# Moving four pieces of work inside the rows of a two-step graph layer

## The chip, the cores and the metric

The kernel runs on one core of a Trainium2 chip, in one launch. The metric is device time in microseconds (us). The engines named below are TensorE (PE, with its weight loads as PEld), VectorE (DVE), ScalarE (ACT), GpSimd (POOL) and SyncE (SP, which issues most DMAs). Each engine runs its own instructions in order and waits for the others through semaphores.

## The reference

3327 nodes with 256 features each; the adjacency matrix has about five entries a row. After a layer norm and a ReLU, two steps of two sums run side by side, and a last layer norm closes. Cut to what matters:

```python
h = maximum(layernorm(x), 0)
R = adj + eye;  R = R / R.sum(-1)            # sparse graph sum
Xf = Xa = h;  Z = 0
for n in range(2):
    probs = softmax((Xa @ W1.T @ W2.T) @ (Xa @ W3.T).T)     # N x N
    keep  = the largest probabilities of each row, until their sum reaches 0.9
    A     = probs * keep / (probs * keep).sum(-1)
    Xf = R @ Xf
    Xa = A @ Xa
    Z  = Z + Xf @ U1[n].T + Xa @ U2[n].T
out = x + layernorm(h + Z)
```

## The kernel before

The nodes are padded to 26 blocks of 128 (`NT`), and a "row" below is one block of 128 nodes against all 3328. For each row of a step the kernel makes the logits on PE and their exponentials on ACT (`weights`, four parts of 832 columns, tile `e`), guesses a threshold with passes over the whole row on ACT (`measured`, L660 to L762, each pass 128x3328 into `ja`), searches the exact threshold on DVE (`settle`, L765: one masked copy of the row at L772, the eight largest of 20 segments at L777, rounds of MAX8 and MATCH_REPLACE at L784 and L788, and the masked row itself at L814), turns the masked row block by block on PE with copies on ACT (`Sums.turn`, L862 and L864), and sums it with the features on PE (`Sums.sum`, L876).

The guess uses a "law", a mean and a variance for each query. In the first step `law_once` makes it row by row: a matmul (L525) and a copy on ACT (L527), and then a product on DVE (L533) and five small operations on POOL (L536 to L540). `weights` calls the first half after the first exponential and the second half after the second.

The graph sum is sparse. In the first step DVE scans the whole adjacency matrix in pieces (`listed`: a DMA into `at`, and a TENSOR_REDUCE at L906) to list the entries of each row; rows from 7 on come in seven pieces of at most 128x512, and each call asks for the next piece's DMA ahead of its own reduction, in two buffers. POOL gathers the listed rows with indirect DMAs (L973 and L990), and `spread` (L1213) sums them: five matmuls into the PSUM tile `pr` (L998), and on DVE L1222, L1224, L1226, L1227 (which reads `pr`) and L1230, then a store to `vx`. `pr` has one buffer, and `first_end` (L1021) uses it next, for the matmuls of L1036.

The order on each engine is written by hand. The loop at the end runs over the rows `i`, and each row has seven slots `k`. A slot's string names generators by letters, and each letter runs one of them to its next `yield`: `m` measured, `d` settle, `c` the rest of the last row's settle, `s` graph sum, `w` logits and exponentials of row i+2, `a` a list piece, `i` the chain that closes a list, `p` and `h` the packing of lists, `g` a gather, `e` and `f` the ends of rows, `b` the products ahead of the first step. `PLAN` (L1249) holds the strings of a common row, `BEGIN` and `OPEN` those of the first rows. In the first step the turning comes behind a slot's letters, in the second in front of them; the sums come last. In the second step slot 1 sums two blocks and slot 2 none (`BLOCKS`), and in slot 2 the first two blocks of the newly masked row are turned. At the end every instruction is tied to the one before it in its engine's queue, so this order is the order on the chip. A gather is also tied to the ACT instruction written last before it.

Of the kernel before, what the change touches and what calls it, by code (L numbers as in the profile page):

```python
# [328 lines left out]
HALVES = 7  # L329
# [17 lines left out]
def guess_graph_layer(ctx, tc, x, adj, w1t, w2t, w3t, u1t, u2t, ln_g, ln_b, out, flag):  # L347
# [18 lines left out]
    valid = lambda t: 0 <= t < NT  # L366
# [148 lines left out]
    def asked(t):  # L515
        qT = tpool.tile([P, P], F32, tag="qT", name="qT", bufs=3)
        for rows in (low, high):
            nc.sync.dma_start(qT[rows], query_of(t))
        return qT

    def law_once(step, t, copy=S.copy):

        pq = ps_t.tile([P, 4, P], F32, tag="pt", name="pq")
        pm = pq[:, 1:3, :].rearrange("p a b -> p (a b)")[:, : 2 * DA + 2]
        PE.matmul(pm, query_of(t), qm[query_at(t), step, :], start=True, stop=True)  # L525
        mq = small.tile([P, 2 * DA + 2], F32, tag="mq", name="mq", bufs=2)
        copy(mq, pm)  # L527
        yield


        ms = small.tile([P, 9], F32, tag="ms", name="ms")
        col = lambda k: ms[:, k : k + 1]
        V.scalar_tensor_tensor(mq[:, : DA + 1], mq[:, : DA + 1], 1.0, mq[:, DA + 1 :], ALU.mult, ALU.mult,  # L533
                               accum_out=col(1))
        minus = mq[:, 2 * DA + 1 :]
        G.tensor_tensor(col(2), col(1), half[:, 1:2], ALU.pow)  # L536
        G.tensor_scalar(ms[:, 3:7], of_s[:, step, :], col(2), 1.0e-4, ALU.mult, ALU.add)
        G.tensor_scalar(col(7), col(1), 0.5, minus, ALU.mult, ALU.subtract)
        G.tensor_scalar(col(7), col(7), 0.25, LNY[step] - 0.25 * math.log(0.1 / N), ALU.mult, ALU.add)
        G.tensor_scalar(col(8), col(1), minus, col(4), ALU.subtract, ALU.add)  # L540
        return col
# [31 lines left out]
    def law_of(t):  # L573

        return lambda k: law[:, {7: 1, 8: 4}.get(k, k), t : t + 1]

    def weights(step, t, live, known=True):

        r = dict(Z=rec[:, step, 3, t : t + 1])
        qT = asked(t)  # L580
        yield
        r["ms"] = law_of(t) if known and step else early.get(t)
        lawful = law_once(step, t) if known and not step else none
        r["e"] = e = es[(2, 3, 0, 1, 4, 5)[t % 6] if step else t % 4]
        r["za"] = za = small.tile([P, CUT + 1], F32, tag="za", name="za")
        live[step, t] = r
        w = HALF * P
        wd = w // CUT
        pls = {}

        def product(n):
            pls[n] = pl = ps_l.tile([P, 2, 512], F32, tag="pl", name="pl")
            for a in range(2):
                p = slice(a * DA, (a + 1) * DA)
                PE.matmul(pl[:, a, :wd], qT[p, :],  # L595
                          keys_of(step, a).rearrange("p a b -> p (a b)")[:, n * wd : (n + 1) * wd],
                          start=True, stop=True)

        for n in range(CUT):
            c = n * wd  # L600
            if n not in pls:
                product(n)
            pl = pls.pop(n)
            if n < CUT - 1:
                S.activation(e.rearrange("p (a n) -> p a n", a=2)[:, :, c : c + wd], pl[:, :, :wd],  # L605
                             AF.Exp, accum_out=za[:, n : n + 1])
                if known and not step and n < 2:
                    r["ms"] = returned(lawful) if n else next(lawful)
                if known and step and n == CUT - 2:
                    product(n + 1)  # L610
                yield
            else:
                S.activation(e.rearrange("p (a n) -> p a n", a=2)[:, :, c : w - 1], pl[:, :, : wd - 1],
                             AF.Exp, accum_out=za[:, n : n + 1])
                S.activation(e[:, w - 1 : w], pl[:, 0, wd - 1 : wd], AF.Exp, accum_out=za[:, n + 1 :])
                if step:
                    r["chain"] = guessing(r)

    def guessing(r):

        r["col"] = col = lambda k, g=small.tile([P, 18], F32, tag="g", name="g"): g[:, k : k + 1]
        ms = r["ms"]
        S.activation(r["za"], r["za"], AF.Copy, accum_out=r["Z"])
        yield
        S.activation(col(0), r["Z"], AF.Ln)
        yield
        S.activation(col(2), col(0), AF.Relu, scale=-0.25, bias=ms(7))
        yield
        S.activation(col(1), col(0), AF.Exp, scale=-1.0, bias=con(5))
        yield  # L630
        S.activation(col(2), col(2), AF.Exp, scale=-1.0, bias=con(9))
        yield
        S.activation(col(3), col(2), AF.Square, bias=con(8))
        yield
        S.activation(col(11), col(2), AF.Square, bias=con(4))  # L635
        S.activation(col(9), col(3), AF.Exp, scale=ms(3), bias=ms(8))

    def guess_of(t):
        for _ in live[1, t]["chain"]:
            yield  # L640
# [16 lines left out]
    def con(k):  # L657
        return one[:, k : k + 1]
# [277 lines left out]
    def chain():  # L936
        while chains:
            if next(chains[0], chains) is chains:
                chains.pop(0)
            yield  # L940
# [133 lines left out]
    def proof():  # L1074
        prove(1)
        yield
        pf = ps_t.tile([P, 4, P], F32, tag="pt", name="pf")
        PE.matmul(pf[:1, 0, :1], fl, ones, start=True, stop=True)
        V.tensor_copy(flag, pf[:1, 0, :1])

    none = iter(())
    chains = []
    own_of, kept, ends = {}, {}, []
    live, ohs, acs, xgs, done, early = {}, {}, {}, {}, [], {}

    def run(work, n=99):
        for _ in range(n):
            next(work, None)

    def returned(work):  # L1090
        while True:
            try:
                next(work)
            except StopIteration as end:
                return end.value
# [29 lines left out]
    lister, product = listed(), products()  # L1125
# [3 lines left out]
    for q in range(HALF + 5):  # L1129
# [31 lines left out]
        if 0 <= q - 1 < HALF:  # L1161
            k, rn = q - 1, scaled.pop(q - 1)
            pt = ps_t.tile([P, 4, P], F32, tag="pt", name="pt")
            for h in range(2):
                t = 2 * k + h
# [70 lines left out]
    def refetch(t):  # L1236
# [8 lines left out]

    ROUNDED = "dsdfdfddfd"
    CLOSED = "zmdmzmzdmmdmdmdmdmd"
    SEARCH = "gmdidsdidadsdg", "gmidpdsdpdidiesa"
    PLAN = (("gmdsssa", "gmcdssa", "edawwpg", *SEARCH, "ohgdeawwqg", "gehmdmdmagq"),  # L1249
            ("llcmnmss", "lms", "lwwnfd", "lcmdssgggg", "fdwmwmqd", "llzmz" + ROUNDED, "l" + CLOSED + "g"))  # L1250

    LAST = {NT - 1: ("cfss", "cn", "nd", "sss", "f" + "d" * 5 + "sdf" + "d" * 11, "ff", ""),
            NT: ("c", "", "", "ff", "ff", "ffv", "f"),
            NT + 1: ("fv", "f", "", "", "f", "f", "f")}
    BEGIN = {-1: ("mba", "mmbba", "mwwbbaa", "bmwwb", "", "", ""),
             0: ("mdbb", "mcdbb", "medbwwbp", "mdbb", "gmpdbwwb", "hgdbgbq", "hgq"),
             1: ("ggmdsssbb", "gmcdgsssbb", "gedbwwbp", "bmsdg", "gmpdeg", "hgdwwqg", "hgemgqo"),
             NT + 1: ("", "weweee", "", "", "", "", ""),
             2: ("gmdsssa", "gmcdssga", "gedawwpg", *SEARCH, "ohgdeawwqg", "gehmdmdmagq")}
    OPEN = {-1: ("mxx", "mxl", "mxlggg", "mgxl", "mwxl", "m" * 7 + "l", "lmlggg"),  # L1260
            0: ("cmmssggg", "lnms", "wwnfd", "cmdss", "fdwmgwmqd", "zmz" + ROUNDED, CLOSED),
            1: ("cmnmss", "ms", "wwnfd", "cmdssgggg", "fdwmwmqd", "zmzg" + ROUNDED, CLOSED + "g")}
    OPEN[2] = OPEN[3] = OPEN[1]
    spacing = itertools.chain(spaced((0, 1)), *(spaced((t,)) for t in range(2, NT)))
    fetching = itertools.chain(*(refetch(t) for t in range(NT)))
# [22 lines left out]
    for step in range(2):  # L1288
        sums = Sums(step, live, xw if step else x0, AHEAD[step])

        for i in range(-1, NT + 2):
            if step == 0 and i == NT - 3:
                begun = [weights(1, t, live, False) for t in range(3)]
            if step == 1 and i == -1:
                ordered.append(len(trace))
            if step == 1 and i == -1:
# [3 lines left out]
                n=work["m"],  # L1300
                c=work["d"],
# [3 lines left out]
                w=later.pop((step, i + 2), none),  # L1305
                z=guess_of(i + 2) if step and i > 0 and valid(i + 2) else none,
                e=first_end(i - 2) if step == 0 and valid(i - 2) else none,
                a=itertools.islice(lister, HALVES) if step == 0 else none, i=chain(),
                p=packed(i + 1) if step == 0 and i >= 0 and valid(i + 1) else none,
                g=fetching if step else spacing if i > -1 else none,  # L1310
                o=asked_for(0, i - 1) if step == 0 and valid(i - 1) else none,
                h=gathered(i) if step == 0 and valid(i) else none,
                b=none if step else product, q=none, v=proof() if step and i == NT else work.get("v", none),
                l=laws(range(3, NT)) if step and i == -1 else work["l"] if step and i == 0 else none,
# [15 lines left out]
            for k in range(PARTS):  # L1330
# [8 lines left out]
                g = PARTS * (i - 1) + k - LATE[step]  # L1339
                summing = valid(g // PARTS)  # L1340
                if step and valid((g + AHEAD[1]) // PARTS):
                    sums.turn(g + (k == 2), min(i, NT - 1))
                for c in ({**OPEN, **LAST} if step else BEGIN).get(i, PLAN[step])[k]:
                    at = len(trace)
# [19 lines left out]
            if step == 1 and i == 0:  # L1364
                for e in es[4:]:
                    G.memset(e[:, N:NP], 0.0)
            for c in ("lcnwqsepb" if i > -1 else "cnwqsepb") if step else "ocmwqseph" + "b" * (i > 0):
                run(work[c])
            if step == 0 and i == NT + 1:
                stores()  # L1370
# [51 lines left out]
```

## Time and profile before

| | us |
|---|---|
| median of 3 runs | 1320.46 |
| lowest and highest | 1314.64, 1323.86 |
| the profiled execution | 1318.03 |
| its span, first to last instruction | 1315.9 |
| mean granted clock of TensorE | 0.982 |
| first step, rows 2 to 25, by the chain of waits | about 130 to 705 |
| between the steps | about 705 to 780 |
| second step | about 780 to 1316 |

The profile is of one execution. A line of its tables has the kernel's line, the engine, the operation, the tiles as out<-in, the shape and the count; then busy time, mean duration in nanoseconds, and the idle time of the engine just before these instructions with what ended it. "issue" means that nothing in the profile shows what ended it. PE's matmuls are pipelined and their ends are modelled, so the spacing of their starts says more than their durations. In a timeline the columns are start, duration, engine, line, operation and tiles, and in brackets the idle time before.

### The profile page before, as it was taken

To read this page: it belongs to the slowest core of one execution; us is meant where nothing else is said; L and a number is where in the kernel's file an instruction comes from. 1 tells how busy PE (TensorE), PEld (TensorE's weight loads), DVE (VectorE), ACT (ScalarE), POOL (GpSimd) and SP (SyncE) were. 2 spreads that over 40 slices of the span, in tenths; PEclk is the share of its full clock that TensorE was granted. 3 is DMA by queue.
4 is the path that set the end of the run, shared out by engine and by line. 5 is a ranking of instruction groups with operands and counts; after the bars stand their busy time and mean duration, and the time that the engine had idled before them with its cause. 6 is when DMAs were issued, how large, how long until landed. Compare 5 with 4: busy or idle time off the path is not lost.

```text
span 1315.9 us, 21931 instructions
## 1 busy us (share of the span) xinstructions
PE 1236.7 (94%) x6292; PEld 935.4 (71%) x6292; DVE 1149.2 (87%) x3830; ACT 1051.4 (80%) x2281; POOL 955.6 (73%) x1201
## 2 busy tenths in 40 slices
PE   5989899999999999999999859999999999999985
PEld 4535677777777777777778537777787777777874
DVE  6867899999999999999685489999999999999993
ACT  5376787787788797887883579999999999999941
POOL 6114888877778878878776367888888888888832
PEclk9999999999999999999999959999999999999998
DMA  7734455555555555553233212222122131221200
GB/s 232 283 127 140 141 147 142 154 154 139 149 145 147 160 148 153 156 139 101 78 97 98 71 48 71 67 71 84 53 85 79 54 89 59 75 85 49 82 21 23
DMA packets 96578, 144.59 MB, mean 110 GB/s; under 512 B 19361, under 2 KB 63008, under 8 KB 96448
## 3 DMA queue, kind: packets, MB, share of 16 engines
q1 hardware_dynamic: 78912, 100.20, 24.3%
q0 software_dynamic: 16640, 42.69, 13.1%
q8 instruction: 52, 0.85, 0.3%
q14 instruction: 78, 0.64, 0.2%
q10 hardware_dynamic: 896, 0.21, 0.1%
HBM read 114.06 MB, written 25.57 MB: 106 GB/s over the span
## 4 chain that ended last, share of the span: by engine, by line
PE 43%; DVE 27%; ACT 22%; issue 3%; DMA 2%; POOL 1%; SPq 0%; ACTq 0%; POOLq 0%; DVEq 0%
PE pa L876 18%; ACT ja L662 11%; PE pl L595 7%; PE pt L862 6%; DVE e L814 5%; DVE cand L777 4%; DVE w L772 3%; DVE fm L906 3%; PE pr L998 3%; ACT e L605 3%; PE pz L1111 3%; PE pz L1036 2%; ACT eT L864 2%; DVE bb L784 2%; DVE x L814 2%
## 5 line engine op out<-in xcount | busy, mean ns | idle before, releaser
L662 ACT ACTIVATE ja<-e,g 128x3328 uint8<-128x3328 f32 x106 | 326.0, 3075 | 0.3
L876 PE MATMUL pa<-xw,eT 128*128 128x256 f32 x1352 | 321.6, 383 | 3.8 <-DVE s L1048 3.8
L876 PE MATMUL pa<-x,eT 128*128 128x256 f32 x1352 | 323.0, 381 | 0.1
L876 PEld LDWEIGHTS pa<-xw,eT 128*128 128x128 f32 x1352 | 251.0, 191 | 49.5 <-issue 13.8
L876 PEld LDWEIGHTS pa<-x,eT 128*128 128x128 f32 x1352 | 243.5, 191 | 26.3 <-ACT xa L885 0.4
L777 DVE MAX8 cand<-w 128x8 f32<-128x168 f32 (+1 forms) x1040 | 253.1, 317 | 0.0
L864 ACT COPY eT<-pt 128x512 f32<-128x512 f32 (+1 forms) x364 | 199.2, 555 | 57.3 <-PE pt L862 50.3
L973 POOL DMA_INDIRECT ac<-in_adj,index x130 | 186.9, 1438 | 60.5 <-issue 29.1
L990 POOL DMA_INDIRECT xg<-bx,index x130 | 180.3, 1387 | 50.3 <-issue 23.8
L862 PE MATMUL pt<-ident,e 128*128 128x128 f32 x1144 | 176.4, 277 | 6.6 <-DVE e L811 2.9
L862 PEld LDWEIGHTS pt<-ident,e 128*128 128x128 f32 x1144 | 139.2, 143 | 60.1 <-issue 36.7
L772 DVE SCALAR_TENSOR_TENSOR w<-e,g 128x3328 f32<-128x3328 f32 x44 | 162.8, 3700 | 0.3
L998 PE MATMUL pr<-xg,ac 128*128 128x257 f32 (+1 forms) x520 | 141.8, 397 | 12.3 <-DVE s L1227 8.1
L990 POOL DMA_INDIRECT xg<-vx,index x130 | 128.4, 987 | 34.2 <-issue 27.6
L814 DVE SCALAR_TENSOR_TENSOR e<-e,rec 128x3328 f32<-128x3328 f32 x40 | 147.2, 3680 | 0.6
L605 ACT ACTIVATE e<-pl 128x832 f32<-128x832 f32 x132 | 114.2, 867 | 27.7 <-PE pl L595 24.3
L998 PEld LDWEIGHTS pr<-xg,ac 128*128 128x128 f32 x520 | 93.8, 195 | 40.1 <-issue 16.9
L595 PE MATMUL pl<-both,qT 64*128 64x416 f32 x416 | 102.2, 549 | 6.9 <-ACT e L605 3.1
L711 POOL TENSOR_SCALAR g<-g,law 128x1 f32<-128x1 f32 x23 | 76.9, 3342 | 22.3 <-ACT g L635 22.1
L906 DVE TENSOR_REDUCE fm<-at 128x4 f32<-128x512 f32 (+1 forms) x133 | 84.7, 637 | 7.9 <-DMA at<-in_adj 5.0
L595 PE MATMUL pl<-after,qT 64*128 64x416 f32 x416 | 89.5, 544 | 0.0
L712 POOL TENSOR_SCALAR g<-g 128x1 f32<-128x1 f32 x26 | 87.0, 3348 | 1.7
(288 smaller groups left out, 2034.9 us busy)
## 6 DMA issues: line engine op xcount, KB each, us to landing
at<-in_adj SPq DMA_DIRECT2D x114, 256.0 KB
cx<-ac SPq DMA_DIRECT2D x26, 320.0 KB
ac<-cx SPq DMA_DIRECT2D x26, 320.0 KB
wide<-in_adj SPq DMA_DIRECT2D x8, 832.0 KB
e<-in_adj SPq DMA_DIRECT2D x6, 832.0 KB
x<-in_x SPq DMA_DIRECT2D x13, 256.0 KB
qT<-both SPq DMA_DIRECT2D x104, 32.0 KB
xr<-in_x SPq DMA_DIRECT2D x26, 128.0 KB
```

What stands on the lines that cost most here:

```text
L595: PE.matmul(pl[:, a, :wd], qT[p, :], keys_of(step, a).rearrange("p a b -> p (a b)")[:, n * wd : (n + 1) * wd], start=True, stop=True)
L605: S.activation(e.rearrange("p (a n) -> p a n", a=2)[:, :, c : c + wd], pl[:, :, :wd], AF.Exp, accum_out=za[:, n : n + 1])
L662: S.activation(ja, e, f, bias=guess, scale=sign, accum_out=total)
L772: V.scalar_tensor_tensor(w, e, col(16), e, ALU.is_lt, ALU.mult, accum_out=d2)
L777: V.max(cand[:, 8 * s : 8 * s + 8], w[:, s * SEG : min(NP, (s + 1) * SEG)])
L814: V.scalar_tensor_tensor(e, e, at(1), e, ALU.is_ge, ALU.mult, accum_out=ra)
L862: PE.transpose(pt[:, j, :], e[:, (j0 + j) * P : (j0 + j + 1) * P], ident)
L864: S.copy(eT[:, :w, :], pt[:, :w, :])
L876: PE.matmul(self.pa, eT[:, c - 4 * k, :], self.xa[:, j, :], start=c == 0, stop=c == NT - 1)
L973: G.indirect_dma_start(out=ac[:, k, :], out_offset=None, in_=rows, in_offset=bass.IndirectOffsetOnAxis(ap=index[:, t, k : k + 1], axis=0), ...
L990: G.indirect_dma_start(out=xg[:, k, :w], out_offset=None, in_=rows, in_offset=bass.IndirectOffsetOnAxis(ap=index[:, t, k : k + 1], axis=0))
L998: PE.matmul(pr[:, :w], ac[:, k, :], xg[:, k, :w], start=k == 0, stop=k == KT - 1)
```

## The change

Four things are moved; no arithmetic is added or removed.

- **The law's product** (first step). The second half of `law_once` is a letter of its own, `u`, near the end of slot 3. Before, it ran in slot 2 with the second `w`.
- **The graph sum** (first step). The last four `s` move from slots 3 and 4 to slots 2 (one), 3 (two) and 4 (one, near its start).
- **The list pieces** (first step). A common row has six `a`, not seven: that of slot 5 is gone, and those of slots 3 and 4 stand at their ends. Rows 0 and 1 get three and four, and the lists end two rows later, in row 22.
- **The first logits** (second step). The two `w` of slot 2 stand at the end of slot 1, after the slot's pass and graph matmul, and ahead of its two blocks of sums.

In row 0 and row 1 a `p` is also called once more in slot 4, where the end of the row ran it before.

```diff
             if n < CUT - 1:
                 S.activation(e.rearrange("p (a n) -> p a n", a=2)[:, :, c : c + wd], pl[:, :, :wd],
                              AF.Exp, accum_out=za[:, n : n + 1])
-                if known and not step and n < 2:
-                    r["ms"] = returned(lawful) if n else next(lawful)
+                if known and not step and n == 0:
+                    r["lawful"] = lawful
+                    next(lawful)
...
+    def law_end(t):
+        live[0, t]["ms"] = returned(live[0, t].pop("lawful"))
+        yield
...
-    SEARCH = "gmdidsdidadsdg", "gmidpdsdpdidiesa"
-    PLAN = (("gmdsssa", "gmcdssa", "edawwpg", *SEARCH, "ohgdeawwqg", "gehmdmdmagq"),
-            ("llcmnmss", "lms", "lwwnfd", "lcmdssgggg", "fdwmwmqd", "llzmz" + ROUNDED, "l" + CLOSED + "g"))
+    SEARCH = "gmdsdidsdiduadg", "gmidpdsdpdidiea"
+    PLAN = (("gmdsssa", "gmcdssa", "edawwspg", *SEARCH, "ohgdewwqg", "gehmdmdmagq"),
+            ("llcmnmss", "lmsww", "lnfd", "lcmdssgggg", "fdwmwmqd", "llzmz" + ROUNDED, "l" + CLOSED + "g"))
...
-             0: ("mdbb", "mcdbb", "medbwwbp", "mdbb", "gmpdbwwb", "hgdbgbq", "hgq"),
-             1: ("ggmdsssbb", "gmcdgsssbb", "gedbwwbp", "bmsdg", "gmpdeg", "hgdwwqg", "hgemgqo"),
+             0: ("mdbb", "mcdbba", "medbwwbp", "mdbba", "gmppdbwwb", "hgdbgbqa", "hgq"),
+             1: ("ggmdsssbba", "gmcdgsssbba", "gedbwwbp", "bmusdga", "gmppdeg", "hgdwwqga", "hgemgqo"),
...
-             2: ("gmdsssa", "gmcdssga", "gedawwpg", *SEARCH, "ohgdeawwqg", "gehmdmdmagq")}
+             2: ("gmdsssa", "gmcdssga", "gedawwspg", *SEARCH, "ohgdewwqg", "gehmdmdmagq")}
...
-            0: ("cmmssggg", "lnms", "wwnfd", "cmdss", "fdwmgwmqd", "zmz" + ROUNDED, CLOSED),
-            1: ("cmnmss", "ms", "wwnfd", "cmdssgggg", "fdwmwmqd", "zmzg" + ROUNDED, CLOSED + "g")}
+            0: ("cmmssggg", "lnmsww", "nfd", "cmdss", "fdwmgwmqd", "zmz" + ROUNDED, CLOSED),
+            1: ("cmnmss", "msww", "nfd", "cmdssgggg", "fdwmwmqd", "zmzg" + ROUNDED, CLOSED + "g")}
...
-                a=itertools.islice(lister, HALVES) if step == 0 else none, i=chain(),
+                a=itertools.islice(lister, 6) if step == 0 else none, i=chain(),
+                u=law_end(i + 2) if step == 0 and i > 0 and valid(i + 2) else none,
...
-            for c in ("lcnwqsepb" if i > -1 else "cnwqsepb") if step else "ocmwqseph" + "b" * (i > 0):
+            for c in ("lcnwqsepb" if i > -1 else "cnwqsepb") if step else "ocmwuqseph" + "b" * (i > 0):
```

## The prediction

> **What bounds the kernel now.** I read the page first: the shares of busy time and the chain that ended last.
>
> ```profile
> PE 1236.7 (94%) x6292; PEld 935.4 (71%) x6292; DVE 1149.2 (87%) x3830; ACT 1051.4 (80%) x2281; POOL 955.6 (73%) x1201
> ...
> PE 43%; DVE 27%; ACT 22%; issue 3%; DMA 2%; POOL 1%; SPq 0%; ACTq 0%; POOLq 0%; DVEq 0%
> ```
>
> No engine is alone on the chain, so a share says little. The next view is the table of windows, cut into rows of the first step (from one start of TensorE's L959 to the next). Columns after the length: busy time of PE, PEld, DVE, ACT, POOL, then granted clock and DMA.
>
> ```profile
> 180.69:205.48 24.79, 23.16 (x122) 17.68 (x120) 23.05 (x78) 19.95 (x47) 20.16 (x23) 1.00 0.56 155
> 426.98:450.07 23.09, 23.09 (x122) 17.69 (x120) 22.95 (x78) 19.73 (x47) 18.80 (x23) 1.00 0.57 157
> ...
> 474.43:498.11 23.68, 23.16 (x121) 17.69 (x120) 23.54 (x78) 19.83 (x47) 19.39 (x23) 1.00 0.56 152
> 498.11:522.48 24.37, 23.96 (x128) 18.22 (x127) 23.63 (x78) 19.95 (x49) 19.75 (x24) 1.00 0.54 151
> 593.82:618.09 24.27, 23.86 (x128) 18.30 (x127) 21.35 (x73) 19.95 (x49) 19.27 (x24) 1.00 0.35 101
> 618.09:640.98 22.89, 22.89 (x121) 17.77 (x120) 18.60 (x61) 19.73 (x47) 17.35 (x21) 1.00 0.31 86
> ```
>
> Short rows and long rows alternate (every second row has the extra Gram matmuls). A short row that waits for nothing takes 23.09 with PE busy throughout. 24.79 and 23.68 are the same work plus a wait. The long row is 24.37 with PE 23.96, and stays 24.27 when the list pieces have ended and DVE has fallen to 21.35. So PE is the floor, and DVE stands at 23.0 to 23.6, close enough to push PE. Where it pushes is in the table of lines for 156 to 704 us (busy, mean ns | idle before, and what ended it):
>
> ```profile
> L1036 PE MATMUL pz<-u,xT 128*128 128x512 f32 x88 | 43.7, 619 | 7.8 <-DVE s L1227 5.6 <-DVE drs L1226 2.0
> ...
> L525 PE MATMUL pq<-qm,both 64*128 64x130 f32 x42 | 10.2, 324 | 4.5 <-ACT eT L864 4.1 <-issue 0.4
> ```
> ```profile
> L906 DVE TENSOR_REDUCE fm<-at 128x4 f32<-128x512 f32 (+1 forms) x128 | 81.3, 635 | 7.9 <-DMA at<-in_adj 5.0 <-issue 2.8
> L533 DVE SCALAR_TENSOR_TENSOR mq<-mq 128x65 f32<-128x65 f32 x21 | 4.7, 225 | 21.8 <-ACT mq L527 21.8
> ```
>
> PE loses 7.8 us before L1036, which takes the PSUM bank that the graph sum's L1227 reads, and 4.5 us before L525, on ACT's copies. DVE loses 21.8 us before the law's product L533 and 7.9 us before list pieces; that makes L1227 late.
>
> The second step's rows are 20.09 or 20.26 us:
>
> ```profile
> 824.18:844.27 20.09, 20.01 (x104) 15.68 (x105) 18.89 (x65) 19.29 (x40) 17.84 (x21) 1.00 0.28 80
> 864.51:884.77 20.26, 20.02 (x105) 15.68 (x105) 19.02 (x65) 19.35 (x40) 17.18 (x20) 1.00 0.24 72
> ```
>
> PE is the floor here too, with one stop a row, at the transposes of the masked row. The timeline of one row, then the waits of 800 to 1250 us (total, times, longest):
>
> ```profile
> 1043.62 3.43 PEld L876 LDWEIGHTS pa<-xw,eT 128*128 128x128 f32 x16
> 1043.69 3.69 DVE L814 SCALAR_TENSOR_TENSOR e<-e,rec 128x3328 f32<-128x3328 f32 x1
> ...
> 1044.54 3.07 ACT L662 ACTIVATE ja<-e,g 128x3328 uint8<-128x3328 f32 x1
> 1047.30 0.08 DVE L814 DVE_READ_ACCUMULATOR e<-e,rec 128x1 f32 x1
> ...
> 1047.50 0.86 PEld L862 LDWEIGHTS pt<-ident,e 128*128 128x128 f32 x8 [0.45 <-issue]
> ...
> 1047.53 1.06 PE L862 MATMUL pt<-ident,e 128*128 128x128 f32 x8
> 1048.19 1.07 ACT L864 COPY eT<-pt 128x512 f32<-128x512 f32 x2 [0.49 <-PE pt L862]
> ...
> 1048.53 1.67 PE L595 MATMUL pl<-after,qT 64*128 64x416 f32 x8
> ...
> 1049.57 0.86 ACT L605 ACTIVATE x<-pl 128x832 f32<-128x832 f32 x1 [0.30 <-PE pl L595]
> ...
> 1051.74 0.57 PEld L862 LDWEIGHTS pt<-ident,e 128*128 128x128 f32 x4
> 1051.95 0.60 PE L862 MATMUL pt<-ident,e 128*128 128x128 f32 x4
> ```
> ```profile
> PEld pt L862 <- issue: 14.1, 23, 1.7
> ```
>
> The masked row ends at 1047.38, the transposes' weights load at 1047.50, and the first logits, whose inputs were long there, stand behind them.
>
> **The change, part by part.** The profiled execution took 1318.03 us (span 1315.9); the median of three runs is 1320.46 (1314.64 to 1323.86), 2.4 above it. The sum is against 1318.03.
>
> *1. Graph sum earlier, law's product later (first step).* No instruction is added. Old DVE order in one row:
>
> ```profile
> 489.69 0.22 DVE L533 SCALAR_TENSOR_TENSOR mq<-mq 128x65 f32<-128x65 f32 x1
> ...
> 491.10 0.17 DVE L924 MAX8 lists<-fm 128x8 f32<-128x26 f32 x1
> 491.22 0.09 DVE L788 MATCH_VALUE_LOAD cand<-bb,cand 128x8 f32 x1
> ...
> 491.52 0.68 DVE L906 TENSOR_REDUCE fm<-at 128x4 f32<-128x512 f32 x1
> ...
> 493.59 0.48 DVE L1227 SCALAR_TENSOR_TENSOR s<-pr,rrs,s 128x256 f32<-128x256 f32 x1
> ```
>
> In the new letters only two of the rounds' MAX8 and one MATCH_REPLACE stand in front of L1227. L533 (0.14 us of DVE), L924 (0.12), one replace (0.30) and nearly all between the piece at 491.52 and L1227 (2.07, less some 0.17 for the graph sum's own L1224 and L1226) go behind it: about 2.5 us earlier, and any wait at L533 no longer stands in front of it. PE's longest wait before L1036 is 2.49 (a row below), the others are shorter. I take all 7.8 us as gained; the lower end is 0, if something else holds that matmul.
>
> L533 itself comes some 2.5 us later in DVE's order, so most of its 21.8 us of waiting is filled with rounds; DVE then runs against PE, and I count nothing for it. Behind L533 stand, on POOL, five small law operations, and they are moved past two gathers (the last g of slot 2, the first of slot 3), which then go first. POOL is busy 18.8 to 20.2 us of a row, the law is read only in the next row, so 0. L1222 is asked for about one slot earlier and needs the five graph matmuls of slots 0 and 1; they lie before it on PE, cost 0, and if a gather were late DVE would now stand there. The store to vx comes earlier with the sum, in the same order on SP.
>
> *2. The clock.* After one long wait the granted clock drops:
>
> ```profile
> 349.23 2.50 PE L1036 MATMUL pz<-u,xT 128*128 128x512 f32 x4 [2.49 <-DVE s L1227]
> ```
> ```profile
> 349.00:351.00 2.00, 1.77 (x4) 0.91 (x5) 2.00 (x11) 0.42 (x2) 1.39 (x3) 0.89 0.13 35
> 351.00:354.00 3.00, 3.00 (x9) 2.20 (x8) 3.00 (x1) 0.96 (x2) 2.92 (x2) 0.50 0.78 189
> ```
>
> 3.00 us at 0.50 lose 1.5 us of PE. Take the wait away and this goes: 1.5 gained (0 to 1.5). The Trainium skill, "TensorE: Matmul & The Clock Gate", Part 1, says that the clock halves after at least one idle window of about 3.4 us. By that rule 2.49 us of idle would not be the cause, the 1.5 would stay, and the total would be 1.5 us higher. The trace has no other idle stretch just before it, so I go by the rows.
>
> *3. Six list pieces a row instead of seven.* In the table above a piece is 635 ns with its forms, some 0.6 of DVE's time. Nineteen rows lose one each (the one of slot 5, just after the masked row); with PE as floor this is worth nothing in itself, but DVE falls to about 23.0, under 23.1, so it stops pushing PE. The seven pieces that go to rows 0 and 1, and twelve that go to two rows behind, are paid in DVE time. Behind: 18.60 + 6 x 0.6 and about 1 us of its chain is 23.2 against 22.89, in one row: 0.3 lost. In front the cover is DVE's waiting:
>
> ```profile
> 87.53 1.29 DVE L1117 COPY e<-pz 128x512 f32<-128x512 f32 x2 [0.33 <-PE pz L1111]
> ...
> 95.84 0.21 DVE L692 TENSOR_SCALAR g<-g 128x1 f32<-128x1 f32 x1 [4.64 <-ACT g L687]
> ...
> 119.91 0.23 DVE L533 SCALAR_TENSOR_TENSOR mq<-mq 128x65 f32<-128x65 f32 x1 [3.66 <-ACT mq L527]
> ```
>
> Seven pieces are 4.2 us; uncovered they cost 4.2. One stands in front of a copy for which PE waits, with 0.33 of cover (0.3 late); the rest fall into the 4.64 and 3.66. Their seven loads of 256 KB are issued on SP between the stores of the products' rows. I take 1.0 (0 to 4.2).
>
> *4. First logits one slot earlier (second step).* The four logit pairs take 1.6 us of PE (L595, 1048.53 to 1050.12 in the timeline) and now stand before the two blocks of sums: the transposes come 1.6 us later than now, when the masked row has ended. How much of PEld's 14.1 us is waiting? Undisturbed, the weights load 0.21 ahead of the matmul (1051.74, 1051.95); at the wait 0.03 (1047.50, 1047.53). So each of the 23 stops overstates by about 0.2: 14.1 - 23 x 0.2 = 9.5 us, or 0.24 to 0.4 a row. On ACT the two exponentials (0.86 each and a read of 0.2) move between a 3.07 us pass and the copies of the transposes; the gaps of 0.49 and 0.30 in front of copy and exponential close. What is late next: ACT needs 19.3 us a row, DVE 18.9, PE 20.09 - 0.24 = 19.85. PE stays the floor by 0.5 us. Gained 9.5 (lower end 0, if ACT's order puts the wait elsewhere). The loads of the queries are issued a row ahead on SP; nothing of them moves.
>
> The sum: -7.8 - 1.5 + 0.3 + 1.0 - 9.5 = -17.5 us, 1300.5 against the profiled execution, and with the median 2.4 above it, 1303.
>
> **The rivals.**
>
> *One half only.* PE's wait at L1036 goes but reappears before L525, where ACT's copies already cost 4.5; or the second step's wait moves to ACT. Then 9.3 or 9.5 is missing: about 1312. For it: ACT is within 0.5 us of PE in the second step. Against: ACT's order in the first step is not touched, and in the short row of 23.09 neither wait stands.
>
> *Hidden anyway.* Both waits are ends of a loop through DVE that is as slow without them; 1318 to 1321. For it: DVE is at 23.54 in a row of 23.68. Against: DVE also loses a piece a row, and the row of 23.09 shows that PE can run through.
>
> *More.* L525's wait goes too: 1303 - 4.5 = 1298.5. Nothing in ACT's order speaks for it but the relief of a less lagging DVE.
>
> *Slower.* The two exponentials in front of the copies in the second step. Now the copies of the two transposes end at 1049.26, and the next transposes, which reuse their PSUM banks, load at 1051.74: 2.5 us in hand. The exponentials put 2 x (0.86 + 0.2) = 2.1 us in front, less the 0.8 of closed gaps; some 1.2 stays in hand. If ACT comes later than that, PE pays the excess in 24 rows: at 1 us too late +24, and with the 8.0 of the first step 1320.5 + 24 - 8 = 1336. It decides from 0.33 us too late (8.0 / 24). Against: ACT has 0.8 of idle a row, all of it at those two gaps.
>
> **How the numbers follow.** Forecast 0.54, one half only 0.22, more 0.10, hidden anyway 0.07, slower 0.07. A measurement of this kernel, with three runs over 0.7%, tells about 1% from no change: the bounds are 1307.3 and 1333.7. Forecast (1297 to 1308) and more are faster, less 0.02 for the forecast's edge: 0.62. One half, hidden and that 0.02 are same: 0.31. Slower 0.07. The range takes in the forecast, one half and most of more: 1295 to 1314; left out are hidden, slower and the edge of more, under 0.2.
>
> **What would show it.** Step 1: PE's idle before L1036 in the table of lines falls from 7.8 to under 1, DVE's before L533 from 21.8 to a few us, short rows are all near 23.1, long ones still 24.4 with L525's 4.5. Step 2: no window at 0.50 in the middle of the first step. Step 3: pieces two rows longer, no wait of PE for the products' copies beyond today's. Step 4: rows of 19.85, no stop of PEld at L862, ACT's exponentials straight behind the pass. It is wrong if the short rows stay at 23.7, if ACT's wait before copies or PE's before L525 grows, or if the second step's rows stay above 20.

## The result, and the profile after

| | before | after |
|---|---|---|
| median, us | 1320.34 (4 runs, 1314.64 to 1323.86) | 1300.11 (4 runs, 1299.68 to 1305.93) |
| the profiled execution | 1318.03 | 1300.47 |
| its span | 1315.9 | 1298.4 |

The ratio is 0.9861, with a 95% interval of 0.9816 to 0.9906: the changed kernel is faster by 0.9 to 1.8%.

In the changed kernel the code after the new function stands five lines lower: L1227, L1036, L998, L862, L906 of before are L1232, L1041, L1003, L867, L911 now; L525, L533 and L595 keep their numbers. The page's shares and its chain:

```profile
PE 1230.6 (95%) x6292; PEld 936.3 (72%) x6292; DVE 1137.1 (88%) x3830; ACT 1048.6 (81%) x2281; POOL 962.9 (74%) x1201
...
PE 77%; ACT 9%; DVE 9%; issue 2%; DMA 1%; POOL 1%; SPq 0%; POOLq 0%; ACTq 0%; DVEq 0%
```

The shares hardly moved. The chain did: it stood 43% on PE and 27% on DVE, and now it runs through PE for 77%.

Where the 17.5 us of span went shows in the table of windows, with four stages cut alike in both kernels: the front to the start of row 2 (the first matmul of L959, now L964), from there to the start of row 25, the stretch from there up to the first masked row of the second step, and the second step. Before:

```profile
0.00:156.32 156.32, 130.13 (x584) 80.60 (x585) 116.76 (x360) 96.50 (x207) 65.23 (x176) 0.99 0.58 184
156.32:708.16 551.84, 539.53 (x2819) 413.29 (x2818) 514.00 (x1696) 445.28 (x1076) 441.43 (x501) 1.00 0.49 138
708.16:800.25 92.09, 74.21 (x335) 52.18 (x334) 53.62 (x248) 61.32 (x126) 47.90 (x73) 0.85 0.25 70
800.25:1315.90 515.65, 492.82 (x2558) 389.36 (x2556) 464.83 (x1527) 448.28 (x873) 401.04 (x452) 0.99 0.22 65
```

After:

```profile
0.00:157.14 157.14, 130.73 (x584) 80.74 (x585) 123.81 (x380) 96.65 (x207) 65.87 (x173) 0.99 0.64 199
157.14:696.00 538.86, 534.34 (x2819) 413.68 (x2818) 497.62 (x1675) 444.58 (x1076) 449.43 (x505) 1.00 0.48 137
696.00:791.15 95.15, 76.10 (x329) 52.11 (x328) 53.68 (x249) 61.45 (x126) 46.99 (x73) 0.84 0.23 65
791.15:1298.40 507.25, 489.40 (x2563) 389.77 (x2561) 462.00 (x1527) 445.96 (x873) 400.63 (x452) 0.99 0.23 66
```

The front is 0.8 longer, the rows of the first step 13.0 shorter, the stretch between the steps 3.1 longer, the second step 8.4 shorter. Of the change only the second step's first logits of row 0 lie in the third stage, near its end (769.66 us); what made it longer comes before them and is taken up at the end of the part on the prediction.

Rows of the first step after the change, in the same view:

```profile
157.14:181.41 24.27, 23.86 (x127) 18.30 (x126) 22.13 (x76) 19.96 (x49) 20.77 (x25) 1.00 0.49 142
181.41:204.31 22.90, 22.90 (x121) 17.78 (x120) 22.02 (x76) 19.75 (x47) 19.36 (x23) 1.00 0.50 151
...
628.82:653.09 24.27, 23.86 (x127) 18.30 (x126) 19.64 (x71) 19.96 (x49) 20.64 (x27) 1.00 0.30 82
```

Up to the start of row 23 each row takes 24.27 or 22.90 (or 22.89), the values that before were reached only where the list pieces had ended. A falling DVE (22.13, then 19.64) changes nothing any more. The groups of 156 to 704 us, of PE and of DVE:

```profile
L1041 PE MATMUL pz<-u,xT 128*128 128x512 f32 x88 | 41.3, 592 | 0.0
L525 PE MATMUL pq<-qm,both 64*128 64x130 f32 x42 | 10.2, 324 | 4.5 <-ACT eT L869 4.5
```
```profile
L911 DVE TENSOR_REDUCE fm<-at 128x4 f32<-128x512 f32 (+1 forms) x121 | 76.9, 636 | 0.0
...
L533 DVE SCALAR_TENSOR_TENSOR mq<-mq 128x65 f32<-128x65 f32 x21 | 4.7, 223 | 11.8 <-ACT mq L527 11.8
```

PE's 7.8 us before the products is gone, and the products themselves became shorter, from a mean of 619 to 592 ns. L525's 4.5 us stands as it was.

Two rows of the second step, and then a part of the timeline of one:

```profile
1015.77:1035.59 19.82, 19.82 (x106) 15.65 (x105) 19.25 (x64) 19.68 (x40) 17.65 (x20) 1.00 0.26 74
1035.59:1055.41 19.82, 19.82 (x105) 15.65 (x104) 18.82 (x64) 19.22 (x39) 17.22 (x20) 1.00 0.25 74
```
```profile
1030.43 1.67 PE L595 MATMUL pl<-after,qT 64*128 64x416 f32 x8
...
1033.54 0.08 DVE L819 DVE_READ_ACCUMULATOR e<-e,rec 128x1 f32 x1
...
1033.85 0.84 ACT L605 ACTIVATE x<-pl 128x832 f32<-128x832 f32 x1
...
1035.37 1.01 PEld L867 LDWEIGHTS pt<-ident,e 128*128 128x128 f32 x8
1035.59 1.04 PE L867 MATMUL pt<-ident,e 128*128 128x128 f32 x8
1036.22 1.07 ACT L869 COPY eT<-pt 128x512 f32<-128x512 f32 x2 [0.60 <-PE pt L867]
...
1037.98 0.58 PEld L867 LDWEIGHTS pt<-ident,e 128*128 128x128 f32 x4
```

The masked row ends at 1033.62, the transposes load their weights 1.75 us later and 0.22 ahead of their matmul, as undisturbed ones do. PE is busy through the whole row. ACT's copies end at 1037.29, 0.7 before the next transposes load. In the waits of 800 to 1250 us PEld's stop at the transposes has shrunk from 14.1 us to this:

```profile
PEld pt L867 <- issue: 0.4, 2, 0.2
```

### The profile page after: what moved, and what is told of

It is laid out like the page before. It is cut to its first block, busy times and chain, and to the rows that moved or that the text cites. A ratio compares the mean times of both kernels' runs of the same rounds, so it can differ in the third digit from the quotient of the medians.

```text
span 1298.4 us, 21925 instructions
## 1 busy us (share of the span) xinstructions
PE 1230.6 (95%) x6292; PEld 936.3 (72%) x6292; DVE 1137.1 (88%) x3830; ACT 1048.6 (81%) x2281; POOL 962.9 (74%) x1201
## 3 DMA queue, kind: packets, MB, share of 16 engines
q1 hardware_dynamic: 78912, 100.20, 24.7%
## 4 chain that ended last, share of the span: by engine, by line
PE 77%; ACT 9%; DVE 9%; issue 2%; DMA 1%; POOL 1%; SPq 0%; POOLq 0%; ACTq 0%; DVEq 0%
PE pa L881 39%; PE pl L595 11%; PE pt L867 10%; PE pr L1003 6%; ACT ja L667 4%; PE pz L1041 3%; DVE w L777 2%; PE pz L1116 2%; DVE cand L782 2%; ACT eT L869 1%; PE pk L1160 1%; PE pk L485 1%; DMA x<-in_x 1%; DVE fm L911 1%; PE pq L525 1%
## 5 line engine op out<-in xcount | busy, mean ns | idle before, releaser
L978 POOL DMA_INDIRECT ac<-in_adj,index x130 | 170.5, 1312 | 63.2 <-issue 26.6
L867 PE MATMUL pt<-ident,e 128*128 128x128 f32 x1144 | 175.2, 275 | 4.8 <-ACT eT L869 4.2
L867 PEld LDWEIGHTS pt<-ident,e 128*128 128x128 f32 x1144 | 139.4, 143 | 54.0 <-issue 21.5
L995 POOL DMA_INDIRECT xg<-bx,index x130 | 135.1, 1040 | 48.8 <-issue 20.0
L995 POOL DMA_INDIRECT xg<-vx,index x130 | 128.3, 987 | 34.3 <-issue 27.7
L1003 PE MATMUL pr<-xg,ac 128*128 128x257 f32 (+1 forms) x520 | 139.1, 392 | 11.9 <-DVE s L1232 8.0
L1003 PEld LDWEIGHTS pr<-xg,ac 128*128 128x128 f32 x520 | 93.6, 194 | 25.4 <-DVE s L1232 8.7
L595 PE MATMUL pl<-both,qT 64*128 64x416 f32 x416 | 101.9, 547 | 7.7 <-DVE e L1122 3.5
L595 PE MATMUL pl<-after,qT 64*128 64x416 f32 x416 | 89.9, 546 | 0.0
L911 DVE TENSOR_REDUCE fm<-at 128x4 f32<-128x512 f32 (+1 forms) x133 | 84.8, 637 | 3.0 <-DMA at<-in_adj 3.0
```

The lines of the kernel that those rows point to most:

```text
L595: PE.matmul(pl[:, a, :wd], qT[p, :], keys_of(step, a).rearrange("p a b -> p (a b)")[:, n * wd : (n + 1) * wd], start=True, stop=True)
L867: PE.transpose(pt[:, j, :], e[:, (j0 + j) * P : (j0 + j + 1) * P], ident)
L978: G.indirect_dma_start(out=ac[:, k, :], out_offset=None, in_=rows, in_offset=bass.IndirectOffsetOnAxis(ap=index[:, t, k : k + 1], axis=0), ...
L995: G.indirect_dma_start(out=xg[:, k, :w], out_offset=None, in_=rows, in_offset=bass.IndirectOffsetOnAxis(ap=index[:, t, k : k + 1], axis=0))
L1003: PE.matmul(pr[:, :w], ac[:, k, :], xg[:, k, :w], start=k == 0, stop=k == KT - 1)
```

## The experiments

The runs were made in three groups, each beside runs of the kernel before: 1319.73 us (median of 10) for the first four kernels, 1319.08 (17) for the next four, 1316.04 (9) for the last two. "Rows 2 to 24" below is the time from the start of row 2 to that of row 24 in the profiled execution: 531.4 before, 518.4 after.

**Each part by itself.** First the graph sum alone:

```diff
-    SEARCH = "gmdidsdidadsdg", "gmidpdsdpdidiesa"
-    PLAN = (("gmdsssa", "gmcdssa", "edawwpg", *SEARCH, ...
+    SEARCH = "gmdsdidsdidadg", "gmidpdsdpdidiea"
+    PLAN = (("gmdsssa", "gmcdssa", "edawwspg", *SEARCH, ...
```

> Before, with the graph sum's four DVE steps alone moved forward (seven pieces a row, the law's product where it was). In the span from row 2's L959 matmul to the last row's, before has 531.4 us and after 518.4. Theory 'order' (PE waits because L1227 stands behind the search's rounds): PE's idle before L1036 falls from 7.8 to under 1.5, that span to about 520, the time by about 10 to 1310. Rival 'load' (DVE has too much work in a row): DVE still needs 23.5 us a row and the wait comes back within a few rows: idle of 4 or more, span above 526, time within 5 of before. Rival 'law' (DVE's wait at L533 is what delays it): idle of 4 or more as well, with L533's 21.8 us of waiting left.

It took 1305.97 us (1304.98 to 1309.0), ratio 0.9899 (0.9869 to 0.9929). PE has no idle time before L1036, and rows 2 to 24 take 518.5; the second step is as before. For the first step this one edit is enough.

```profile
L1036 PE MATMUL pz<-u,xT 128*128 128x512 f32 x88 | 41.4, 592 | 0.0
```

Then the law's second half alone, with the function and the letter of the change, behind the rounds of slot 3:

```diff
-    SEARCH = "gmdidsdidadsdg", "gmidpdsdpdidiesa"
+    SEARCH = "gmdidsdiduadsdg", "gmidpdsdpdidiesa"
```

> Before, with the law's product alone moved behind. Theory 'order': DVE's wait at L533 falls from 21.8 to under 10, but L1227 stands behind the rounds as before, so PE keeps 2 to 5 us of idle before L1036; span of rows 2 to 24 about 526, time 1315. Rival 'law': idle under 1.5, span about 520, time 1310. Rival 'load': idle unchanged near 7.8, span 530.

It took 1310.73 us (1307.9 to 1312.14), ratio 0.992 (0.9891 to 0.995), rows 2 to 24 in 520.6. DVE's wait at L533 is 15.9, not under 10 as the theory of the order had it, and the time and the span are nearest to what the rival "law" gave. PE's group in the table of lines:

```profile
L1041 PE MATMUL pz<-u,xT 128*128 128x512 f32 x91 | 43.0, 594 | 1.6 <-DVE s L1232 1.6
```

Then six pieces a row alone, with rows 0 and 1 as in the change:

```diff
-    PLAN = (..., *SEARCH, "ohgdeawwqg", "gehmdmdmagq"),
+    PLAN = (..., *SEARCH, "ohgdewwqg", "gehmdmdmagq"),
...
-                a=itertools.islice(lister, HALVES) if step == 0 else none, i=chain(),
+                a=itertools.islice(lister, 6) if step == 0 else none, i=chain(),
```

> Before, with six list pieces a row alone (three and four in rows 0 and 1, the lists two rows longer). Theory 'order': DVE's need falls by 0.6 us a row, but in the short rows L1227 still stands behind the rounds and DVE waits longer at L533, so 2 to 5 us of PE's idle before L1036 stay; span about 525, time 1314. Rival 'load': idle under 1.5, span about 520, time 1310. Both: row 2 begins about 0.8 us later than before, as in the changed kernel.

It took 1311.19 us (1308.89 to 1313.24), ratio 0.9925 (0.9895 to 0.9955), rows 2 to 24 in 521.4, with PE's idle time as the rival "load" gave it, and DVE's wait at L533 at 27.6:

```profile
L1036 PE MATMUL pz<-u,xT 128*128 128x512 f32 x90 | 44.1, 611 | 0.5 <-DVE s L1227 0.5
```

Both of these did far more than they would if only the order of DVE's work counted. Any one of the three edits brings rows 2 to 24 within 3 us of the 518.4. The mean of 611 ns in the last row also shows how a wait hides: the recorded idle is 0.5, yet the rows are 3.0 above those of the full change, and the matmuls look longer.

And the second step's logits alone:

```diff
-             ("llcmnmss", "lms", "lwwnfd", ...
+             ("llcmnmss", "lmsww", "lnfd", ...
```

> Before, with the second step's first logits alone moved forward. My theory: rows of the second step fall from 20.09 and 20.26 to 19.82, the weight loads of the transposes have no idle time left, and the first step keeps its 531.4; 8.9 us gained, time about 1311. Rival (ACT's order takes the wait): rows stay above 20.0, less than 3 us gained.

It took 1309.79 us (1306.22 to 1314.47, 7 runs), ratio 0.9922 (0.9895 to 0.9948). From its first masked row to its last the second step takes 456.9 us against 465.5, 8.6 less. Rows 2 to 24, with an unchanged order, took 526.6 here against 531.4 in the profile of before: the old first step is not the same in every execution, and a row of 27.33 us, with the long wait of 2.49, is in that one only.

**What is needed.** The graph sum and the logits together, without the law and the pieces (the diffs of the first and the fourth run):

> Before, with only the graph sum and the second step's logits moved. If the law's product and the list pieces add nothing once the graph sum is forward: rows 2 to 24 at 518.4 and second-step rows at 19.82, time 1300 within 2, as the changed kernel. If they are needed: rows 2 to 24 above 520 and the time 2 or more above it.

It took 1299.28 us (1299.0 to 1300.56), ratio 0.9858 (0.9834 to 0.9883), rows 2 to 24 in 518.4. That is the whole gain. The other way round, the changed kernel with its graph sum put back where it was:

```diff
-    SEARCH = "gmdsdidsdiduadg", "gmidpdsdpdidiea"
-    PLAN = (("gmdsssa", "gmcdssa", "edawwspg", ...
+    SEARCH = "gmdidsdiduadsdg", "gmidpdsdpdidiesa"
+    PLAN = (("gmdsssa", "gmcdssa", "edawwpg", ...
```

> The changed kernel with the graph sum put back behind the search's rounds; the law, the pieces and the logits as changed. Theory 'any one is enough' (each of the three frees more than the loop through DVE was late, so PE is the floor with any two): rows 2 to 24 within 1 of 518.4, PE's idle before L1036's matmuls under 0.5, time 1300. Theory 'order' as predicted (the graph sum is what takes the wait away): idle of 2 or more and the time 3 or more above the changed kernel.

It took 1299.31 us (1298.55 to 1301.28), ratio 0.9864 (0.9839 to 0.989), rows 2 to 24 in 518.4, and no idle time before L1041. So the law and the pieces together also do the whole of it.

**Is it a loop with a margin?** Call DVE's loop the round of work and waits that brings DVE from a place in one row to the same place in the next. If it was late by a fraction of a microsecond a row, more work on DVE must bring the wait back even with the graph sum in front. In the kernel with the graph sum alone, two of the seven pieces of a row are reduced twice (work is repeated, none is left out). Both are full pieces, which take 0.676 each (the 0.635 of the tables mixes in the smaller last piece), so 1.35 us a row:

```diff
-            V.tensor_reduce(fm[:, j0 : j0 + n], at[:, :n], AX.X, ALU.max, apply_absolute_value=True)
+            for _ in range(2 if t >= HALVES and j0 in (4, 12) else 1):
+                V.tensor_reduce(fm[:, j0 : j0 + n], at[:, :n], AX.X, ALU.max, apply_absolute_value=True)
```

> Before with the graph sum moved forward, and two of the seven list pieces of each row reduced twice (the same result): 1.2 us more of DVE's time in a row. DVE then needs 23.5 + 1.2 = 24.7 us a row against PE's mean of 23.6. If DVE's load becomes the floor from there: rows of 24.7 on average, rows 2 to 24 about 540, time about 1325. If the order alone decides: rows 2 to 24 stay at 518.4, time 1306.

One run took 1323.28 us, and rows 2 to 24 took 533.6. Most rows, short ones as long ones, take about 24.5, and the wait is back at its old place (lines stand one lower than before):

```profile
L1037 PE MATMUL pz<-u,xT 128*128 128x512 f32 x89 | 43.2, 606 | 7.8 <-DVE s L1228 7.7
```

Two rows in the table of windows, a short one and a long one:

```profile
327.67:352.16 24.49, 23.35 (x122) 17.71 (x120) 24.28 (x80) 20.04 (x47) 19.49 (x23) 1.00 0.52 149
352.16:376.66 24.50, 24.05 (x127) 18.29 (x126) 24.33 (x81) 19.94 (x49) 19.84 (x24) 1.00 0.53 149
```

Rows of one length, whether PE has the Gram matmuls or not, with DVE busy for 24.3 of 24.5, mean that DVE's loop sets them. With 1.35 us more it is 24.5, so without them about 23.15, against PE's mean of 518.4 / 22 = 23.56: the graph sum alone leaves an estimated 0.4 us a row in hand. The 533.6 lie between the 540 that was expected for "load" and the 518.4 for the order alone: the loop is 24.5 and not 24.7, and the first two rows and the last four are at PE's length. Before, the mean was 531.4 / 22 = 24.15, so the loop was late by 0.59 us a row, 0.2 of it in the one row of 27.33; in the execution with 526.6 it was late by 0.37.

**L525's 4.5 us.** They remain in every kernel so far, 0.4 in each of 11 long rows. A stretch of the changed kernel's timeline shows the place, and the new order on DVE:

```profile
501.28 0.48 DVE L1232 SCALAR_TENSOR_TENSOR s<-pr,rrs,s 128x256 f32<-128x256 f32 x1
501.36 0.58 ACT L869 COPY eT<-pt 128x512 f32<-128x512 f32 x1
...
501.99 0.38 PE L525 MATMUL pq<-qm,both 64*128 64x130 f32 x1 [0.41 <-ACT eT L869]
...
502.94 0.29 ACT L527 COPY mq<-pq 128x130 f32<-128x130 f32 x1
...
503.25 0.23 DVE L533 SCALAR_TENSOR_TENSOR mq<-mq 128x65 f32<-128x65 f32 x1 [0.84 <-ACT mq L527]
```

L525 takes one of two PSUM banks (`ps_t`) that the transposes use as well, and starts when ACT's copy has emptied it, at 501.94. The first attempt moved the law's first half to the second exponential:

```diff
-                if known and not step and n == 0:
+                if known and not step and n == 1:
```

> The changed kernel, with the first half of the law (its matmul L525 and copy) called after the second part of the logits instead of the first. Theory: L525 waits for an ACT copy of transposes to free a PSUM bank, and one more logit pair (0.9 us of PE) fills the wait: the 4.5 us before it go, long rows fall from 24.27 to 23.80, rows 2 to 24 from 518.4 to about 513.3, time about 5 below the changed kernel's 1300.1: 1295. Rival (ACT's chain of copies and passes is the limit of a long row): the wait turns up before another matmul and rows stay at 24.27.

It took 1317.21 us (1314.31 to 1321.96, 12 runs), ratio 0.9998 (0.9982 to 1.0015): rows 2 to 24 take 535.2, so more was lost than the first step had gained. L525's wait is gone, and a larger one stands at the next user of those banks:

```profile
L867 PE MATMUL pt<-ident,e 128*128 128x128 f32 x588 | 92.7, 277 | 23.0 <-ACT lists L953 23.0
...
L525 PE MATMUL pq<-qm,both 64*128 64x130 f32 x42 | 8.0, 272 | 0.0
```

Now another place for the product, with the order untouched: 130 unused columns of the graph sum's own PSUM tile, in rows above 3. Once with the whole change,

```diff
+        if step == 0 and t > 3:
+            pm = sums_of["pr"][:, 320 : 320 + 2 * DA + 2]
+        else:
+            pq = ps_t.tile([P, 4, P], F32, tag="pt", name="pq")
+            pm = pq[:, 1:3, :].rearrange("p a b -> p (a b)")[:, : 2 * DA + 2]
...
-        pr = ps_r.tile([P, 2 * D], F32, tag="pr", name="pr")
+        pr = sums_of["pr"] = ps_r.tile([P, 2 * D], F32, tag="pr", name="pr")
```

> The changed kernel, with the law's first product of the long rows (t above 3, first step) written into unused columns of the graph sum's PSUM tile instead of a bank of ps_t. Theory bank: the 4.5 us that PE stands still at L525 in the long rows (11 of them, some 0.4 us each) is a wait for a ps_t bank that an ACT copy still reads; with another bank the long rows fall from 24.27 to about 23.8 us, the L525 row shows no idle time, rows 2 to 24 take 513 to 514 us instead of 518.4, and the kernel about 1295. Rival ACT: ACT's own chain sets the long rows, and the wait turns up at the next user of a ps_t bank, as it did where the law's half was moved by itself: the long rows stay at 24.27 or grow, and the time stays at 1299 to 1302 or above.

and once, by the same lines, with the graph sum and the logits alone:

> The kernel before with the graph sum in front of the rounds and the second step's logits alone, and the law's product of the long rows in the unused columns of the graph sum's PSUM tile. Theory bank: long rows about 23.8 us, the time some 4 to 5 us below the 1299.3 of the same kernel without the new place. Rival ACT: long rows 24.27 or more, time 1299 or more. With the law's product at its old place here and behind in the other kernel, the pair also tells whether its place matters once the bank is not shared.

The second gave 1294.93 us (1292.85 to 1295.67, 5 runs), ratio 0.9833 (0.982 to 0.9847), the shortest of all kernels, though its interval overlaps that of the graph sum and the logits without the new place. Its first two rows, and its groups of PE:

```profile
159.16:182.75 23.59, 23.59 (x128) 18.39 (x126) 22.64 (x78) 19.53 (x49) 18.86 (x23) 1.00 0.53 144
182.75:205.44 22.69, 22.69 (x121) 17.86 (x120) 22.55 (x78) 20.00 (x48) 19.12 (x23) 1.00 0.54 156
```
```profile
L1039 PE MATMUL pz<-u,xT 128*128 128x512 f32 x91 | 43.6, 600 | 1.8 <-DVE s L1231 1.7
...
L528 PE MATMUL pr<-qm,both 64*128 64x130 f32 x42 | 8.0, 272 | 0.0
```

Long rows fall by 0.68 and short ones by 0.21, and rows 2 to 24 take 512.2 instead of 518.4. It isn't all PE's floor: 1.8 us of idle time has come back before the products. PE's first two rows average 23.14, rows 2 to 24 average 23.28, and DVE's loop was estimated at 23.15 above: PE is now about as fast as DVE's loop.

The first, with the law's product behind the rounds, started with the same rows of 23.59 and 22.69, and from row 11 on the short rows and some of the long ones are longer, up to 24.82, and one, with the clock halved in it, 27.63; rows 2 to 24 take 520.5. It took 1305.0 us (1303.7 to 1306.09), ratio 0.9913 (0.9898 to 0.9929). In its timeline:

```profile
430.76 0.38 PE L528 MATMUL pr<-qm,both 64*128 64x130 f32 x2
...
432.28 0.29 ACT L530 COPY mq<-pr 128x130 f32<-128x130 f32 x1
...
432.60 0.22 DVE L1231 TENSOR_SCALAR rrs<-pr,dg 128x1 f32<-128x1 f32 x1 [1.29 <-ACT mq L530]
```

DVE's first instruction of the graph sum (L1231, before L1222) reads the same bank as ACT's copy of the law and starts when that copy ends. It now waits 34.3 us in all (next to nothing in the changed kernel), 18.6 of them put down to that copy, and what DVE has behind it waits too. In the other kernel the law's product on DVE is ahead of the graph sum, so that the copy is waited for there (9.6 us in all, in four rows), and the graph sum's first instruction waits for nothing. So the theory of the bank held for L525's wait, and what the shared bank then costs I put down to the place of the law's product in DVE's order. That is read from these waits and not shown by a run that moves the product alone: the two kernels also differ in the list pieces. The Trainium skill, "PSUM — Partial Sum Buffer", Terms, says that two engines may not touch one bank at once, reads against reads included. That agrees with a DVE read that starts 0.03 us after ACT's has ended; whether the program or the chip keeps them apart the trace doesn't show.

## Why the prediction was right

The forecast was faster with 1303 us; it is faster, with 1300.1. Against the profiled execution the sum was -17.5 us, and -17.56 was measured. That agreement is partly luck. By stage -13.0 + 0.8 + 3.1 - 8.4 was measured: the first step gained 4.0 more than forecast, and the stretch between the steps and the logits together took 4.2 of it away again. By the medians the gain is 20.2, since the profiled execution after lies near its median and that of before 2.3 below its own.

- **Graph sum and law, -7.8.** Right that the whole idle time before the products goes. The size was too small: with the halved clock and the list's end, -9.0 was forecast for the first step's rows, and they gained 13.0. The term took PE's recorded idle time alone. The matmuls behind it also became shorter, 619 to 592 ns over 88, 2.4 us, which I read as a part of the wait that the modelled ends hid; one of them, at 1061 ns, belongs to the halved clock. The prediction took 23.09 for a short row that waits for nothing, as PE was busy all through it; undisturbed short rows take 22.90, and long ones 24.27 instead of 24.37. The rest I can't assign. How much of the 13.0 is this one execution's stays open too: against the 526.6 of the other execution with the old order it is 8.2, while the medians of the run with the graph sum alone are 13.8 apart.
- **"About 2.5 us earlier" for L1227** was right for the graph sum alone and too small for the two together. From the start of the row it stood at 18.6 to 21.1 us before in nearly all rows, at 16.6 to 17.8 with the graph sum alone, and stands at 13.6 to 14.3 now (501.28 against the start of that row at 487.32), mostly 5 to 6 us earlier. The sum counted the instructions that changed places and gave no size to the wait at L533, which had stood in front of it. L533 still waits 11.8 us, not a few, but the graph sum now stands ahead of it.
- **"Six pieces, worth nothing in themselves"** was wrong. The run with the pieces alone gained nearly all of the first step. The step assumed that the moved graph sum was what removed the wait; the runs show one loop through DVE, late by about half a microsecond a row, that each of the three edits shortens by about enough. The rival "hidden anyway" was nearer to this mechanism, a loop through DVE, and wrong in its size: without the waits that loop is 0.4 us a row shorter than PE's work, not as slow. The gains of the four kernels with one part each add up to 13.8 + 9.0 + 8.5 + 9.9 = 41.2 us, against 20.2 for the whole. "DVE falls under PE's floor" was right: 22.0 in a short row of 22.90.
- **The front, +1.0, and the list's end, +0.3.** Measured +0.8, but the start of row 2 lies anywhere from 156.3 to 160.5 us in the kernels run, those with the old front among them (156.4 with the graph sum alone, 159.4 with the logits alone), so the cost isn't told apart from none. The list's end cost nothing: the short row that was to grow (618.09 before, 605.93 now) takes 22.89 before and 22.90 now, and the rows behind it are equal too.
- **The clock, -1.5.** Right: there is no halved window between rows 2 and 25. Nor is there one in the run with the logits alone, which has the old first step and no wait of 2.49 us. By the rule of the Trainium skill, "TensorE: Matmul & The Clock Gate", Part 1, that the prediction weighed, the loss would have stayed. Of all twelve kernels only one other has a spell in these rows, the whole change with the law's product in `pr`: 3.41 us at 643.9, behind a stop of PE of 2.14. No other run has a stop of over 2 us there, so the rows are borne out twice; that such a stop doesn't always bring a spell is shown at the end.
- **Logits, -9.5.** Measured -8.4 and, alone, -8.6. Rows of 19.85 were forecast and are 19.82. PEld no longer stops at the transposes, as their timeline shows. The guard against the slower rival, that ACT's copies still come in time, held with 0.7 us in hand instead of 1.2.
- **L525** keeps its 4.5 us, as forecast, and so the rival "more" failed for the change itself. "One half only" failed in both halves.

**The stretch between the steps** was no part of the forecast, and cost 3.1 us. The same PE work ran at half the clock in the changed kernel. Its table of windows:

```profile
728.00:732.00 4.00, 2.60 (x15) 1.88 (x14) 1.88 (x9) 3.97 (x3) 0.25 (x1) 1.00 0.45 137
732.00:735.00 3.00, 3.00 (x10) 1.36 (x10) 1.20 (x12) 1.75 (x2) 2.41 (x7) 0.78 0.21 78
735.00:738.00 3.00, 3.00 (x8) 1.87 (x8) 2.07 (x10) 0.00 (x0) 2.17 (x6) 0.50 0.09 32
738.00:741.00 3.00, 3.00 (x6) 1.00 (x5) 0.30 (x3) 0.00 (x0) 2.39 (x3) 0.58 0.60 161
```

and at full speed in that of before, 12 us later:

```profile
740.00:744.00 4.00, 2.79 (x14) 2.04 (x14) 1.87 (x7) 3.97 (x3) 0.50 (x2) 1.00 0.47 132
744.00:747.00 3.00, 2.81 (x11) 1.45 (x11) 1.54 (x14) 2.10 (x2) 2.17 (x6) 1.00 0.32 121
747.00:750.00 3.00, 3.00 (x13) 1.64 (x13) 2.22 (x12) 0.00 (x0) 2.43 (x6) 1.00 0.18 51
```

In the profiles of the first eight kernels of the experiments this stretch is 91.9 to 92.2 us where no such spell shows (five, the one with the graph sum and the logits among them), 93.6 with one spell of 3.4 us (two), and 95.1 with 6.8 us (six pieces alone), a loss of about half the spell. The last two fit less well: 94.8 with one spell of 3.4, and 93.9 with none set apart. In the kernels with the law alone and with the pieces alone PE, DVE and ACT have the same instructions in the same order here as before, so no moved instruction in the stretch makes the spell. But it came in five of the six kernels in which the law or the pieces are moved and in none of the other six, so these profiles don't tell a part of the change from the execution; what starts a spell stays open.

## What to carry to other kernels

Where an engine runs through a loop that is late by a few tenths of a microsecond a row, several small edits each gain nearly the whole, and their gains don't add up: price the loop's margin, not the edits. When an instruction is moved, count the waits that stood in front of it, and look at the means of the matmuls behind a wait as well as at the recorded idle time. A wait for a buffer goes away only with a place that nobody else in the same loop needs at that time; moved along, it came back five times as long at the next user.

## What the runs showed of the hardware

- Half-clock spells come in lengths of about 3.4 us or its multiples (3.4, 6.8, 10.2). The one after 733 us began behind 4 us in which PE was busy for 2.60, and PE's longest stop just before it is in this row of the timeline:

```profile
731.84 0.93 PE L552 MATMUL pq<-qm,both 64*128 64x130 f32 x6 [1.40 <-DVE mq L527]
```

  The kernel before has the same stop of 1.40 us there, and no spell. A longer stop, 2.35 to 2.38 us near the end of the second step, stands in all twelve kernels (at 1255.02 in the one before): a spell of 3.4 us began within 1.5 us of it in four and in eight not. The Trainium skill, "TensorE: Matmul & The Clock Gate", Part 1, speaks of free-running windows of 3.4 us: the lengths agree, and a free-running window would let the same work be hit in one execution and missed in the next; that it takes an idle window of that length doesn't agree with the 1.40.
- A wait of PE shows in part as idle time and in part as longer matmuls: L525's mean fell from 324 to 272 ns when its bank was no longer shared, 42 x 0.052 = 2.2 us beside the 4.5 recorded. In the first six rows, where no new wait had come up yet, these two make 1.9 of the 2.7 us by which the rows became shorter; the rest I can't assign.
